# A two-layer graph network kernel: layer 0's first group by eight plain outer products instead of seven combined ones, its results in both streams' banks, and first loads in another order

## The chip, the core and the metric

The kernel runs on one core of a Trainium2 chip. The metric is device time in microseconds (us) from the first to the last instruction. Engines work side by side, each with its own queue in order, and wait for one another by semaphores: TensorE (PE, with its weight loads PEld), VectorE (DVE), ScalarE (ACT), GpSimd (POOL) and SyncE (SP), which here only issues transfers. Results of matmuls go to eight banks of PSUM, of 128 partitions by 512 float32 numbers each.

## The reference

There are 128 graphs of 128 nodes with 512 features. Layer 0 gathers neighbours, multiplies by one weight matrix and normalizes; layer 1 is a diffusion over two hops.

```
# layer 0, for each graph b
deg = sum(adj, -1);  agg = (adj @ x) / max(deg, 1e-6)
out = relu(concat([x, agg]) @ W.T)            # W is 512 x 1024
x = layernorm(x + out)
# layer 1, for each graph b
e = leaky_relu(sj + si + ab, 0.2)             # scores from x @ Wv and aw
T = adj * exp(e), rows divided by their sums
h = x @ Wk[0] + T @ (x @ Wk[1] + T @ (x @ Wk[2])) + biases   # the sum over hops, rewritten
x = layernorm(x + relu(h))
```

By linearity layer 0's product is computed as x @ W1 + adj_n @ (x @ W2), where W1 and W2 are the two halves of W.T and adj_n is the adjacency with its rows divided by the degrees.

## The kernel before

**Groups and streams.** The graphs go through in 32 groups of four (G), as two pairs p = 0, 1. Two generators emit the instructions of TensorE and their companions in steps: `stream0` is layer 0 of one group, 18 steps (NA), and `stream1` is layer 1 of one pair, 9 steps, in other banks (bA0 to bA3 for stream 0, bB0 to bB3 for stream 1). The main loop at the end of the file takes one step of each per turn t, stream 1 beginning at t = 24 (LAG). The order on all engines is the order of emission in this loop: it runs as written.

**What stands beside them.** Everything else (loads, transposes, sums, statistics, softmax) is a list of small functions with a place each: place 2t is emitted after stream 0's step t, place 2t + 1 after stream 1's. `EARLY` holds the places of group 0, `PLACES` of the middle groups, `LATE` of the last, each counted from the group's start; `START` holds what happens once (weight sums, folding of constants, the first x sums). What a step appends to `late` is emitted after the place's functions, the evictions of a last bank among them.

**Products.** Both layers' products use a fast scheme with seven products for a 2 by 2 block product (instead of eight), with sums of blocks ahead of it and additions in the banks behind it. Layer 0 uses it twice. The inner level is `prod(bank, k)` for k = 1 to 7 in the order 1, 5, 6, 2, 7, 3, 4, with the tables `LEFT` and `RIGHT` choosing the blocks. The outer level is over pairs of graphs (xu for pair 0, xl for pair 1), halves of the 512 input features, and the two column blocks W2 and W1. It also has seven products, in `outer_pair(1, 2)`, `(5, 6)`, `(7, 4)`, and product 3 by itself (49 block products in all). Its left sums are `x_s1` to `x_s4` (lines 224 to 233), its right sums `w_outer(1)` to `(4)` (line 681), its result sums `sum_s`, `sum_d`, `sum_c21`, `sum_c22` on GpSimd and VectorE. Results go to SBUF (r, s, c11, c22) and the last ones stay in the banks bA, where the products with the transposed adjacency aT (`mm(bA[...], aT[...], ...)`) are added to them. `residual` then adds relu of a bank to y.

**One product in the code.** `mm` (line 251) issues one block product of 128x128 by 128x256; the profile counts two MATMUL instructions for each, so 49 block products are 98 instructions. Between prod 1 and prod 6 ScalarE copies bank 0 to bank 1 (line 263) and bank 3 to s5 (line 265); VectorE adds s5 into bank 2 behind prod 6 (line 268) and into bank 3 behind prod 7 (line 273); TensorE's next product in bank 0 must wait for these additions to have read it.

**x and the weights.** x comes by `load_x_blocks` in 32-row blocks and is turned by VectorE in 32x32 blocks (`x_turn`, line 216), then `x_inner` makes the left inner sums in four additions (lines 202 to 205). wf holds 7 by 7 weight blocks: `load_w0(o)` fills outer index o, raw, `w_inner(p)` makes the inner sums of two outer indices (lines 196 to 199: p = 0 for blocks 0 and 2, p = 1 for blocks 1 and 3), and `w_outer` adds whole outer blocks of 128 x 1792 numbers.

**Start.** 16 matmuls on the identity (line 149) fill the banks; then the first product needs block 0 of the weights and pair 0 of x. The loads at the head of the kernel are 16 transfers of 128 KB for the weights and 8 for x of group 0. The 8 hardware semaphores for transfers are taken in turn: transfer n waits, on the queue that issues it, for transfer n - 8 to have landed. Constants of layer 1 are folded between group 0's products (`fold_constants`, lines 160 to 185; line 180 is the step on VectorE that ends in the vector `w2row`).

Of the kernel before, what the change touches and what calls it, by code (L numbers as in the profile page):

```python
# [8 lines left out]
FP = mybir.dt.float32  # L9
AF = mybir.ActivationFunctionType  # L10
ALU = mybir.AluOpType
# [5 lines left out]
def kernel(  # L17
# [38 lines left out]
    nc = tc.nc  # L56
    P = 128
    B, N, F = x.shape
    K = wk.shape[0]
    NC = F // P  # L60
    H = NC // 2
    FH = F // 2
    G = 4
    NG = B // G
# [4 lines left out]
    p1 = ctx.enter_context(tc.tile_pool(name="p1", bufs=1))  # L69
# [3 lines left out]
    small = ctx.enter_context(tc.tile_pool(name="small", bufs=4))  # L73
# [3 lines left out]
    R = 32  # L77
    Q = P // R
    xbs, adjs, ys = {}, {}, {}
# [14 lines left out]
    def load_x_blocks(g, p):  # L94
        b = g * G + 2 * p
        xbs[g, p] = p2.tile([P, 2, Q, P], FP, name="xb", tag="xb")
        load_blocks(xbs[g, p], x[b : b + 2])

    def load_adj(g):
        adjs[g] = p2.tile([P, G, N], FP, name="ag")  # L100
        nc.sync.dma_start(adjs[g], adj[g * G : (g + 1) * G].rearrange("b i j -> i b j"))


    wf = const.tile([P, 7, 7, FH], FP)
# [4 lines left out]
    ab_sb = const.tile([P, 1], FP)  # L109
    bk_sb = p1.tile([K, F], FP, name="bk_sb", tag="scr")  # L110

    def load_w0(eng, o):
        src = w0t[(F if o in (0, 2) else 0) + 0 :]
        for q in range(Q):
            r0 = q * P + (o // 2) * H * R
            eng.dma_start(wf[q * R : (q + 1) * R, o, :4].rearrange("s (c n) m -> s c (n m)", c=H),
                          src[r0 : r0 + H * R].rearrange("(c s) o -> s c o", s=R))

    load_w0(nc.scalar, 0)
    load_x_blocks(0, 0)  # L120
    load_w0(nc.sync, 2)
    load_w0(nc.scalar, 1)
    load_x_blocks(0, 1)
    load_w0(nc.scalar, 3)
    load_adj(0)
    for i in range(2):
        nc.sync.dma_start(wvt_sb[i], wvt[i * FH : (i + 1) * FH, :].rearrange("(c p) f -> p c f", p=P))
# [18 lines left out]
    bA = [psum.tile([P, F], FP, name=f"bA{i}") for i in range(4)]  # L146
    bB = [psum.tile([P, F], FP, name=f"bB{i}") for i in range(4)]
# [43 lines left out]
    LEFT = [None, 0, 1, 6, 3, 4, 5, 2]  # L191
    RIGHT = [None, 0, 2, 3, 6, 4, 5, 1]
# [8 lines left out]
    def left_sums(eng, t):  # L201
        eng[0].tensor_add(t[4], t[2], t[3])  # L202
        eng[1].tensor_sub(t[2], t[0], t[2])
        eng[2].tensor_sub(t[5], t[4], t[0])  # L204
        eng[3].tensor_sub(t[6], t[1], t[5])

    V, S_, L_ = nc.vector, nc.gpsimd, nc.scalar


    xu = const.tile([P, 2, 7, P], FP)  # L210
    xl = const.tile([P, 2, 7, P], FP)
    xs = const.tile([P, 2, 7, P], FP)

    def x_turn(g, p, i):
        t, src = (xu, xl)[p], xbs[g, p]
        V.transpose(t[:, :, 2 * i : 2 * i + 2].rearrange("p o k (j r) -> p j o k r", r=R),
                    src[:, i].rearrange("p j (o k s) -> p j o k s", o=2, k=2))

    def x_inner(g, p):
        t = (xu, xl)[p]  # L220
        left_sums([V, V, V, V], [t[:, :, i] for i in range(7)])
# [13 lines left out]
    def left_of(i):  # L235
        return {1: xu[:, 0], 2: xu[:, 1], 3: xu[:, 1], 4: xl[:, 1], 5: xs[:, 0], 6: xs[:, 1], 7: xl[:, 0]}[i]

    def right_of(i):
        return wf[:, RIGHT[i]]
# [10 lines left out]
    def mm(dst, lhsT, rhs, start=False):  # L250
        nc.tensor.matmul(dst, lhsT, rhs, start=start, stop=True, skip_group_check=True)  # L251


    ans, aTs, ybs, yfs, scs, Ts, TTs = {}, {}, {}, {}, {}, {}, {}
# [27 lines left out]
    late = []  # L282
# [4 lines left out]
    def stream0(g):  # L287

        r = p1.tile([P, 4, FH], FP, name="r")
        c11 = p1.tile([P, 4, FH], FP, name="c11")  # L290
        s = p1.tile([P, 4, FH], FP, name="s")
        d = p1.tile([P, 3, FH], FP, name="d")
        c22 = p1.tile([P, 4, FH], FP, name="c22")
        parts[g] = r, s, d, c22

        def evict1(b):
            L_.copy(r[:, b], bA[b][:, :FH])
            V.tensor_add(c11[:, b], bA[b][:, FH:], r[:, b])
        yield from outer_pair(1, 2, evict1)

        def evict2(b):
            L_.copy(s[:, b], bA[b][:, :FH])  # L302
            V.tensor_add(r[:, b], bA[b][:, FH:], r[:, b])  # L303
        yield from outer_pair(5, 6, evict2)

        def evict3(b):
            L_.copy(c22[:, b], bA[b][:, :FH])  # L307
            V.tensor_add(r[:, b], bA[b][:, FH:], r[:, b])  # L308
        yield from outer_pair(7, 4, evict3)


        X, Y, W, Z, E = bA[2][:, :FH], bA[1][:, :FH], bA[1][:, FH:], bA[2][:, FH:], bA[3][:, :FH]
        def prod(dst, k):
            mm(dst, left_of(3)[:, LEFT[k]], right_of(3)[:, RIGHT[k]])
        s5 = p1.tile([P, 2, FH], FP, name="hs")
        L_.copy(X, s[:, 0])
        L_.copy(E, d[:, 1])
        prod(X, 1)
        V.tensor_add(Y, X, d[:, 0])
        prod(E, 5)  # L320
        L_.copy(s5[:, 0], E)
        yield
        prod(Y, 2)
        V.tensor_add(s5[:, 1], s5[:, 0], d[:, 2])
        prod(X, 6)
        V.tensor_add(W, X, s5[:, 0])
        yield
        prod(X, 7)
        V.tensor_add(Z, X, s5[:, 1])
        prod(W, 3)  # L330
        L_.copy(bA[0].rearrange("p (a m) -> p a m", a=2), c22[:, 1:3])  # L331
        yield
        prod(X, 4)
        L_.copy(bA[3].rearrange("p (a m) -> p a m", a=2), c22[:, 0:4:3])
        yield
        own, other = slice(1, 3), slice(0, 4, 3)
        aT = aTs[g]
        mv = mvs[g] = small.tile([P, G, 2], FP, name="mv")
        def residual(b, k):
            y = ys[g, b // 2][:, b % 2]  # L340
            V.scalar_tensor_tensor(y, bA[k], 0.0, y, ALU.max, ALU.add, accum_out=mv[:, b, 0:1])
        mm(bA[0], aT[:, 2], r[:, own])
        mm(bA[3], aT[:, 3], r[:, other])
        late.append((residual, 2, 0))
        late.append((residual, 3, 3))
        yield
        mm(bA[1], aT[:, 0], c11[:, own])
        mm(bA[2], aT[:, 1], c11[:, other])
        late.append((residual, 0, 1))
        late.append((residual, 1, 2))  # L350
        yield

    parts = {}

# [24 lines left out]
    mvs, rstds = {}, {}  # L379
# [243 lines left out]
    def x_s1_next(): pass  # L623
    nexts = {load_adj_next: load_adj, load_x_blocks_next: load_x_blocks, x_turn_next: x_turn, x_inner_next: x_inner, x_s1_next: x_s1}

    EARLY = {
        (t_load,): 42, (t_back,): 51, (y_store, 1): 43, (y_turn, 1, 0): 46, (load_x, 0): 0, (x_s4,): 6, (sum_s,): 17,
        (sum_c21,): 23, (sum_c22,): 25, (a_transpose,): 25, (load_adj_next,): 5, (load_x_blocks_next, 1): 9,
        (x_turn_next, 1, 1): 23, (x_turn_next, 0, 1): 33, (y_stats, 2): 34, (x_turn_next, 1, 0): 26, (y_stats, 3): 33,
        (y_scales, 1): 34, (y_scores, 2): 33, (o_store, 0): 90, (y_norm, 2): 35, (y_norm, 3): 35, (y_store, 2): 36,  # L630
        (t_norm,): 49, (y_store, 3): 36, (y_stats, 0): 37, (y_stats, 1): 38, (x_turn_next, 0, 0): 28,
        (y_scales, 0): 40, (y_scores, 0): 35, (y_scores, 1): 39, (y_norm, 0): 40, (y_norm, 1): 40, (y_store, 0): 41,
        (x_inner_next, 1): 30, (y_load, 0): 44, (t_scores,): 40, (t_exp,): 47, (t_sums,): 48, (t_transpose,): 55,
        (y_turn, 1, 1): 46, (y_sums, 1): 47, (y_turn, 0, 0): 57, (y_turn, 0, 1): 60, (y_sums, 0): 64,
        (o_stats, 1): 66, (o_scales, 1): 66, (o_norm, 1): 69, (o_store, 1): 72, (o_stats, 0): 84, (o_scales, 0): 87,
        (x_inner_next, 0): 33, (y_scores, 3): 33, (load_x, 1): 13, (sum_d,): 22, (y_load, 1): 38,
        (load_x_blocks_next, 0): 25, (o_norm, 0): 87, (x_s1_next,): 33,
    }
    PLACES = {
        (o_scales, 0): 87, (y_norm, 1): 42, (x_turn_next, 1, 1): 27, (o_store, 1): 73, (o_norm, 0): 87, (x_s4,): 11,  # L640
# [35 lines left out]
    def w_inner(p):  # L676
        right_sums([V, V, V, V], [wf[:, p : p + 3 : 2, i] for i in range(7)])

    def w_outer(i):
# [1 line left out]
        eng.tensor_sub(wf[:, d], wf[:, m], wf[:, n])  # L681

    START = {
        (x_turn, 0, 1, 0): 1, (x_inner, 0, 1): 2, (x_s2, 0): 5, (w_outer, 4): 10, (degree, 0): 8, (fold, 3): 2,
        (fold, 4): 15, (fold, 5): 9, (load_wk,): 11, (fold, 2): 5, (x_turn, 0, 1, 1): 1, (w_inner, 1): 0,
        (fold, 1): 6, (w_outer, 3): 12, (w_outer, 2): 3, (fold, 7): 23, (wk_sums, 0): 24, (wk_sums, 2): 45,
        (x_s1, 0): 3, (fold, 6): 5, (a_load, 0): 17, (a_norm, 0): 12, (x_s3, 0): 6, (w_outer, 1): 0,
    }
    for (f, *args), place in START.items():
        at(place, f, *args)  # L690
    for i in range(2):
        x_turn(0, 0, i)
    w_inner(0)
    x_inner(0, 0)

    def run(fs):
        while fs:
# [3 lines left out]
    def chain(gens):  # L701
        for h in gens:
            yield from h()

    a = chain([lambda g=g: stream0(g) for g in range(NG)])
    b = chain([lambda g=g, p=p: stream1(g, p) for g in range(NG) for p in (1, 0)])
    ET = mybir.EngineType
    with tc.manual_schedule(engines={ET.PE, ET.DVE, ET.Activation, ET.Pool, ET.SP}):
# [34 lines left out]
```

## Time and profile before

| | us |
|---|---|
| median of 3 runs | 2235.78 (2235.29 to 2237.61) |
| profiled execution | 2235.6 |
| PE busy | 2197.9 (98%) |
| VectorE busy | 1378.6 (62%) |
| ScalarE busy | 1060.2 (47%) |
| GpSimd busy | 690.9 (31%) |
| PE busy in the first 100 us | 75.22 |
| mean granted TensorE clock | 0.995 |

PE's busy time tells at most where it is not busy: the share says little on how well it computes. The slices of the page show where along the run an engine is short of work; the list of waits says what ended each idle time; the timeline puts these in order. In the timeline each line begins with the start and the length of a run of like instructions, and the brackets tell how long the engine was idle before it and what released it. DMA lines on a queue give the time of issue only.

### The profile page before, as it was taken

To read this page: it belongs to the slowest core of one execution; us is meant where nothing else is said; L and a number is where in the kernel's file an instruction comes from. 1 tells how busy PE (TensorE), PEld (TensorE's weight loads), DVE (VectorE), ACT (ScalarE), POOL (GpSimd) and SP (SyncE) were. 2 spreads that over 40 slices of the span, in tenths; PEclk is the share of its full clock that TensorE was granted. 3 is DMA by queue.
4 is the path that set the end of the run, shared out by engine and by line. 5 is a ranking of instruction groups with operands and counts; after the bars stand their busy time and mean duration, and the time that the engine had idled before them with its cause. 6 is when DMAs were issued, how large, how long until landed. Compare 5 with 4: busy or idle time off the path is not lost. (4 is left out here: it accounts for less than half of the span.)

```text
span 2235.6 us, 24900 instructions
## 1 busy us (share of the span) xinstructions
PE 2197.9 (98%) x7520; PEld 1424.9 (64%) x7520; DVE 1378.6 (62%) x3219; ACT 1060.2 (47%) x2438; POOL 690.9 (31%) x983
## 2 busy tenths in 40 slices
PE   7899999999999999999999999999999999999998
PEld 4566666666666666666666666666666666666654
DVE  5766665666665666665666655666656666656652
ACT  2444444544445544445545445444445544455443
POOL 3432323332322322322322232323233223223221
PEclk8999999999999999999999999999999999999999
DMA  8333344333344333344333344333443233443321
GB/s 188 95 95 98 82 104 123 110 85 103 89 105 123 104 86 89 97 117 123 93 92 87 97 123 113 90 97 88 104 123 109 81 102 92 109 123 98 87 81 47
DMA packets 392039, 226.60 MB, mean 101 GB/s; under 512 B 155357, under 2 KB 335581, under 8 KB 391904
## 3 DMA queue, kind: packets, MB, share of 16 engines
q1 hardware_dynamic: 390816, 223.43, 38.0%
q10 hardware_dynamic: 960, 1.57, 0.4%
q8 instruction: 59, 0.97, 0.2%
q14 instruction: 76, 0.62, 0.1%
q0 software_dynamic: 128, 0.01, 0.0%
HBM read 140.52 MB, written 84.41 MB: 101 GB/s over the span
## 5 line engine op out<-in xcount | busy, mean ns | idle before, releaser
L251 PE MATMUL bB<-wk_sb,yf 128*128 128x512 f32 (+1 forms) x2048 | 723.5, 486 | 3.5 <-DVE bB L550 1.7
L251 PE MATMUL bB<-t,yf 128*128 128x512 f32 (+1 forms) x1536 | 558.0, 486 | 1.0 <-ACT bB L517 1.0
L251 PEld LDWEIGHTS bB<-wk_sb,yf 128*128 128x128 f32 x2048 | 388.6, 190 | 238.6 <-issue 200.3
L251 PEld LDWEIGHTS bB<-t,yf 128*128 128x128 f32 x1536 | 291.9, 190 | 192.8 <-issue 161.1
L251 PE MATMUL bA<-wf,xu 128*128 128x256 f32 x1344 | 340.4, 386 | 15.8 <-DVE bA L268 6.4
L204 POOL TENSOR_TENSOR yf<-yf 128x256 f32<-128x256 f32 x64 | 57.8, 903 | 926.6 <-DVE yf L202 910.6
L251 PEld LDWEIGHTS bA<-wf,xu 128*128 128x128 f32 x1344 | 252.1, 192 | 119.5 <-issue 60.3
L251 PE MATMUL bA<-wf,xs 128*128 128x256 f32 x896 | 216.2, 382 | 4.9 <-DVE bA L268 3.5
L251 PEld LDWEIGHTS bA<-wf,xl 128*128 128x128 f32 x896 | 169.9, 190 | 78.9 <-issue 58.4
L251 PE MATMUL bA<-wf,xl 128*128 128x256 f32 x896 | 214.6, 380 | 1.0 <-DVE r L303 1.0
L251 PEld LDWEIGHTS bA<-wf,xs 128*128 128x128 f32 x896 | 171.1, 191 | 56.7 <-issue 28.9
L268 DVE TENSOR_TENSOR bA<-bA,hs 128x512 f32<-128x512 f32 x96 | 67.1, 699 | 190.9 <-PE bA L251 186.5
L391 DVE SCALAR_TENSOR_TENSOR scr<-y,wrow 128x512 bf16<-128x512 f32 x256 | 177.0, 691 | 5.5
L377 ACT ACTIVATE junk<-y,mvo 128x512 bf16<-128x512 f32 x128 | 92.4, 722 | 142.4 <-POOL mvo L376 136.8
L331 ACT COPY bA<-c 128x512 f32<-128x512 f32 x32 | 18.9, 590 | 250.2 <-DVE y L562 235.2
L308 DVE TENSOR_TENSOR r<-bA,r 128x256 f32<-128x256 f32 x128 | 48.4, 419 | 139.7 <-ACT c L307 137.3
L404 ACT ACTIVATE y<-y,mv,sc 128x512 f32<-128x512 f32 x128 | 104.9, 822 | 62.1 <-POOL mv L398 61.6
L251 PE MATMUL bB<-v,TT 128*128 128x512 f32 x256 | 130.8, 592 | 0.0
L562 DVE SCALAR_TENSOR_TENSOR y<-bB,y 128x512 f32<-128x512 f32 x128 | 88.0, 688 | 59.0 <-PE bB L251 58.9
L251 PE MATMUL bB<-u,TT 128*128 128x512 f32 x256 | 120.6, 593 | 0.5 <-DVE TT L501 0.5
L303 DVE TENSOR_TENSOR r<-bA,r 128x256 f32<-128x256 f32 x128 | 48.3, 418 | 116.9 <-ACT s L302 116.9
L357 POOL TENSOR_TENSOR s<-s,r 128x1024 f32<-128x1024 f32 x32 | 75.6, 2363 | 115.1 <-DVE r L303 115.1
(140 smaller groups left out, 2891.1 us busy)
## 6 DMA issues: line engine op xcount, KB each, us to landing
xb<-in_x_dram SPq DMA_DIRECT2D x256, 128.0 KB
y<-in_x_dram SPq DMA_DIRECT2D x64, 512.0 KB
yd<-y SPq DMA_DIRECT2D x128, 256.0 KB
yb<-yd SPq DMA_DIRECT2D x256, 128.0 KB
out_dram<-y SPq DMA_DIRECT2D x128, 256.0 KB
ag<-in_adj_dram SPq DMA_DIRECT2D x32, 256.0 KB
sd<-an SPq DMA_DIRECT2D x32, 256.0 KB
anb<-sd SPq DMA_DIRECT2D x128, 64.0 KB
```

What stands on the lines that cost most here:

```text
L204: eng[2].tensor_sub(t[5], t[4], t[0])
L251: nc.tensor.matmul(dst, lhsT, rhs, start=start, stop=True, skip_group_check=True)
L268: V.tensor_add(bA[2], bA[0], s5)
L303: V.tensor_add(r[:, b], bA[b][:, FH:], r[:, b])
L308: V.tensor_add(r[:, b], bA[b][:, FH:], r[:, b])
L331: L_.copy(bA[0].rearrange("p (a m) -> p a m", a=2), c22[:, 1:3])
L357: S_.tensor_add(s, s, r)
L377: L_.activation(junk, t, AF.Square, bias=mv[:, 0:1], accum_out=mv[:, 1:2])
L391: V.scalar_tensor_tensor(scr, y, 1.0, wrow[:, t], ALU.mult, ALU.mult, accum_out=scs[g][:, t, b : b + 1])
L404: L_.activation(t, t, AF.Identity, bias=mv[:, 0:1], scale=rstd)
L562: V.scalar_tensor_tensor(r, bB[1 + i], 0.0, r, ALU.max, ALU.add, accum_out=mv[:, i, 0:1])
```

## The change

Group 0 of layer 0 gets a generator of its own, `first0`, also of 18 steps. It takes eight outer products without combined sums: for each of the two column blocks (o = 0 for W2, o = 1 for W1) the products of both pairs with both halves of the features are accumulated, `prod` now being four block products (two pairs times two feature halves). A bank's left half holds pair 0, the right half pair 1. So the sums `x_s1` to `x_s4`, `sum_s`, `sum_d`, `sum_c21`, `sum_c22` are not needed for group 0, and the outer weight sums are needed from group 1 on only. Column 0 is evicted to SBUF (c11 and r); column 1 is evicted to the banks bB, which stream 1 does not use yet, and the adjacency products are added there.

The outer weight sums move to later places, and so does `w_inner(1)`. Both pairs of x are turned ahead of the loop. Of the loads, weight block 2 is split over the scalar and the sync queue, and block 1 comes after the second pair of x. Places of group 0's and group 1's other functions shift by a few steps. The purpose is to let TensorE start on raw blocks sooner, with less work of the other engines ahead of it.

```diff
-    def load_w0(eng, o):
+    def load_w0(engs, o):
...
-            eng.dma_start(wf[q * R : (q + 1) * R, o, :4].rearrange("s (c n) m -> s c (n m)", c=H),
+            engs[q % len(engs)].dma_start(wf[q * R : (q + 1) * R, o, :4].rearrange("s (c n) m -> s c (n m)", c=H),
...
-    load_w0(nc.scalar, 0)
+    load_w0([nc.scalar], 0)
     load_x_blocks(0, 0)
-    load_w0(nc.sync, 2)
-    load_w0(nc.scalar, 1)
+    load_w0([nc.scalar, nc.sync], 2)
     load_x_blocks(0, 1)
-    load_w0(nc.scalar, 3)
+    load_w0([nc.scalar], 1)
+    load_w0([nc.scalar], 3)
...
+    def first0():
+        c = [p1.tile([P, 4, FH], FP, name=n) for n in ("c11", "r")]
+
+        def outer_column(o, bank_of, evict):
+            bank = [bA[i] for i in bank_of]
+            def prod(b, k, start=False):
+                for h in range(2):
+                    for i in range(2):
+                        mm(bank[b][:, h * FH : (h + 1) * FH], (xu, xl)[h][:, i, LEFT[k]], wf[:, 2 * i + o, RIGHT[k]],
+                           start and i == h == 0)
+            s5 = p1.tile([P, F], FP, name="hs")
+            prod(0, 1, True)
+            L_.copy(bank[1], bank[0])
+            yield
+            prod(3, 5, True)
+            L_.copy(s5, bank[3])
+            yield
+            prod(0, 6)
+            V.tensor_add(bank[2], bank[0], s5)
+            yield
+            prod(1, 2)
+            yield
+            prod(0, 7)
+            evict(1, bank[1])
+            V.tensor_add(bank[3], bank[0], s5)
+            yield
+            prod(2, 3)
+            yield
+            prod(0, 4)
+            evict(3, bank[3])
+            evict(2, bank[2])
+            late.append((evict, 0, bank[0]))
+            yield
+
+        def evict0(b, t):
+            L_.copy(c[0][:, b], t[:, :FH])
+            V.tensor_copy(c[1][:, b], t[:, FH:])
+        yield from outer_column(0, (0, 1, 2, 3), evict0)
+
+        def evict1(b, t):
+            i, h = {1: (0, 0), 2: (0, 1), 0: (1, 0), 3: (1, 1)}[b]
+            L_.copy(bB[i][:, h * FH : (h + 1) * FH], t[:, :FH])
+            V.tensor_copy(bB[2 + i][:, h * FH : (h + 1) * FH], t[:, FH:])
+        yield from outer_column(1, (1, 2, 0, 3), evict1)
...
+        for p in (1, 0):
+            for i, k in enumerate((slice(1, 3), slice(0, 4, 3))):
+                b = 2 * p + i
+                mm(bB[b], aT[:, b], c[p][:, k])
+                late.append((residual, b))
+                yield
...
     START = {
-        (x_turn, 0, 1, 0): 1, (x_inner, 0, 1): 2, (x_s2, 0): 5, (w_outer, 4): 10, (degree, 0): 8, (fold, 3): 2,
-        (fold, 4): 15, (fold, 5): 9, (load_wk,): 11, (fold, 2): 5, (x_turn, 0, 1, 1): 1, (w_inner, 1): 0,
-        (fold, 1): 6, (w_outer, 3): 12, (w_outer, 2): 3, (fold, 7): 23, (wk_sums, 0): 24, (wk_sums, 2): 45,
-        (x_s1, 0): 3, (fold, 6): 5, (a_load, 0): 17, (a_norm, 0): 12, (x_s3, 0): 6, (w_outer, 1): 0,
+        (w_outer, 4): 18, (degree, 0): 12, (fold, 3): 8, (fold, 4): 11, (load_wk,): 11, (fold, 2): 5, (w_inner, 1): 5,
+        (fold, 1): 9, (w_outer, 3): 28, (w_outer, 2): 11, (fold, 7): 16, (wk_sums, 0): 24, (wk_sums, 2): 45,
+        (fold, 6): 15, (a_load, 0): 17, (a_norm, 0): 13, (w_outer, 1): 9, (fold, 5): 9,
     }
...
-    a = chain([lambda g=g: stream0(g) for g in range(NG)])
+    a = chain([lambda g=g: stream0(g) if g else first0() for g in range(NG)])
```

Of the places of `EARLY`, these move: `x_turn_next` of pair 1 from 26 and 23 to 22 and 28 (halves 0 and 1), the second one of pair 0 from 33 to 31, `x_inner_next(1)` from 30 to 29, `y_scores` of graphs 0 and 1 from 35 and 39 to 38, `y_norm(3)` from 35 to 36.

More of the change, by code (lines that the diff above doesn't have):

```diff
@@ L351, in stream0, with residual @@
         yield
+    def first0():
[39 more added lines that the diff above has]
+        yield from outer_column(1, (1, 2, 0, 3), evict1)
+        aT = aTs[0]
+        mv = mvs[0] = small.tile([P, G, 2], FP, name="mv")
+        def residual(b):
+            y = ys[0, b // 2][:, b % 2]
+            V.scalar_tensor_tensor(y, bB[b], 0.0, y, ALU.max, ALU.add, accum_out=mv[:, b, 0:1])
+        for p in (1, 0):
[4 more added lines that the diff above has]
+                yield
     parts = {}
@@ L626 @@
     EARLY = {
[L627 to L637, printed above, removed]
+        (t_load,): 42, (t_back,): 51, (y_store, 1): 43, (y_turn, 1, 0): 46, (load_x, 0): 0, (a_transpose,): 25,
+        (load_adj_next,): 5, (load_x_blocks_next, 1): 9, (x_turn_next, 1, 1): 28, (x_turn_next, 0, 1): 31,
+        (y_stats, 2): 34, (x_turn_next, 1, 0): 22, (y_stats, 3): 33, (y_scales, 1): 34, (y_scores, 2): 33,
+        (o_store, 0): 90, (y_norm, 2): 35, (y_norm, 3): 36, (y_store, 2): 36, (t_norm,): 49, (y_store, 3): 36,
+        (y_stats, 0): 37, (y_stats, 1): 38, (x_turn_next, 0, 0): 28, (y_scales, 0): 40, (y_scores, 1): 38,
+        (y_norm, 0): 40, (y_norm, 1): 40, (y_store, 0): 41, (x_inner_next, 1): 29, (y_load, 0): 44, (t_scores,): 40,
+        (t_exp,): 47, (t_sums,): 48, (t_transpose,): 55, (y_turn, 1, 1): 46, (y_sums, 1): 47, (y_turn, 0, 0): 57,
+        (y_turn, 0, 1): 60, (y_sums, 0): 64, (o_stats, 1): 66, (o_scales, 1): 66, (o_norm, 1): 69, (o_store, 1): 72,
+        (o_stats, 0): 84, (o_scales, 0): 87, (x_inner_next, 0): 33, (y_scores, 3): 33, (load_x, 1): 13,
+        (y_load, 1): 38, (load_x_blocks_next, 0): 25, (o_norm, 0): 87, (x_s1_next,): 33, (y_scores, 0): 38,
     }
@@ L692 @@
         x_turn(0, 0, i)
+    for i in range(2):
+        x_turn(0, 1, i)
+    x_inner(0, 0)
+    x_inner(0, 1)
     w_inner(0)
-    x_inner(0, 0)
     def run(fs):
```

## The prediction, on record before the run

> **What bounds the kernel now.** I read the granted clock of the core (0.995), then the busy rows by slice, then TensorE's waits, then the timeline of the first 100 us. The rows of the page (tenths of 55.9 us slices):
>
> ```profile
> PE   7899999999999999999999999999999999999998
> PEclk8999999999999999999999999999999999999999
> ```
>
> TensorE is short of full only in the first two slices and the last. Asked by window, TensorE's waits from 100 to 2100 us are none, and from 2100 us on they sum to 4.8 us. In the first 100 us it idles 24.8 us (busy 75.22). So the kernel is TensorE-bound but for its start, and a microsecond won before 100 us moves the end by a microsecond. Waits of the whole run (total, times, longest):
>
> ```profile
> PE bA L251 <- DVE bA L268: 9.9, 2, 6.4
> PE bA L251 <- ACT bA L263: 4.0, 1, 4.0
> ```
>
> TensorE's timeline (start, length, instructions, idle before and its releaser):
>
> ```profile
> 13.35 3.70 PE L251 MATMUL bA<-wf,xu 128*128 128x256 f32 x14 [1.40 <-DMA wf<-in_w0t_dram]
> ...
> 24.49 3.78 PE L251 MATMUL bA<-wf,xu 128*128 128x256 f32 x8 [6.39 <-DVE bA L268]
> ...
> 63.90 1.88 PE L251 MATMUL bA<-r,aTt 128*128 128x512 f32 x4
> ...
> 74.21 6.46 PE L251 MATMUL bA<-wf,xu 128*128 128x256 f32 x20 [4.04 <-ACT bA L263]
> 82.09 1.13 PE L251 MATMUL bA<-wf,xs 128*128 128x256 f32 x4 [1.42 <-DVE c L298]
> ```
>
> Group 0's aggregation starts at 63.90, group 1's second pair at 82.09; from there only 0.97 us is lost up to 2150. These two times are my marks. VectorE's timeline gives the cause:
>
> ```profile
> 17.95 0.69 DVE L196 TENSOR_TENSOR wf<-wf 128x512 f32<-128x512 f32 x1 [1.99 <-DMA wf<-in_w0t_dram]
> ...
> 22.55 1.30 DVE L216 STREAM_TRANSPOSE xl<-xb 128x512 f32<-128x512 f32 x2
> 23.77 0.67 DVE L268 TENSOR_TENSOR bA<-bA,hs 128x512 f32<-128x512 f32 x1
> ...
> 39.36 3.27 DVE L180 TENSOR_SCALAR w2row<-w2row,wm 2x512 f32<-2x512 f32 x1
> ```
>
> The addition that TensorE awaits at 24.4 stood behind the sums of weight blocks 1 and 3, whose loads land at 17.95, behind the outer sum of line 681 (2.02) and two transposes. From 62.9 to 82.0 VectorE does not rest: the windows 60-70 and 70-80 show it 9.65 and 9.60 of 10 us busy, TensorE only 7.26 and 5.96.
>
> **What the Trainium skill says.** "TensorE: Matmul & The Clock Gate", What's actually happening: an idle window of about 3.4 us halves TensorE's clock and a busy one restores it. The trace agrees on the first and is worse on the second: after the 6.39 us wait the clock is 0.50 from 25 to 33.3, the 8 instructions take 0.47 us each, and some 4.3 us are lost; after the 4.04 us wait the 20 instructions take 6.46 instead of 4.9. "SBUF — State Buffer", Who interferes with whom: a VectorE instruction with two SBUF inputs, or in a two-port mode, waits until a running GpSimd instruction ends. It agrees: line 180's 3.27 us ends with GpSimd's 3.96 us sum of 38.39. "DMA: Bandwidth & Descriptors", Issuing engines are not separate DMA queues: a second queue saves issue time only. Here eight loads are in flight and each issue waits for the eighth before it, so the order decides what lands first.
>
> **The change part by part.**
>
> *TensorE's work.* 8 products of 7 block products instead of 7: 56 against 49, two instructions each. 28 such took 6.81 us (48.81 to 55.62), 0.243 each: 14 more are +3.4 us, fully on TensorE's path. The adjacency products keep 4 pairs of instructions.
>
> *Loads.* In before the third block of 4 loads (weight block 2, all on the sync queue) was issued from 4.42 to 8.72 and landed by 13.3, so an issue takes some 4.5 us to land. Now two of these go on the scalar queue, whose next slots were 4.07 and 5.6: block 2 lands near 10.5. The second x pair then takes sync's slots 7.5, 8.7, 10.1 and 10.9 and lands near 15.4 (10.9 + 4.5). The scalar queue gets 14 issues for 12; its last reuses a slot of the x pair, so it ends near 15.5 instead of 13.1. The table load (1.28) follows: ScalarE's first copy can run from 17.0, before that nothing asks for it. Blocks 1 and 3 land near 20, and are wanted only by column 1 of the weights.
>
> *Start.* TensorE does half the first product at 11.5, behind its warm-up, then waits for the second x pair: 15.4 + 1.3 (two transposes) + signal = 16.9. From there to group 0's aggregation: (112 - 4) instructions x 0.243 = 26.2; the folding matmuls between them 0.95 + 0.5 + 3.6 + 2.1 = 7.15 (lines 160, 168, 173, 184 at full clock); half clock after 4.4 us idle, between 1.6 and 4.4 us by the two cases above, taken as 3.0. Sum 36.4, so aggregation starts at **53.3** instead of 63.9, 10.6 earlier.
>
> *Waits inside that stretch.* The first addition into bank 2 (line 268 in before) now stands behind nothing but x sums. Blocks 1 and 3 are summed after it, while TensorE has 2 products of 1.94. The outer sums (VectorE 2.0, GpSimd 2 x 3.96) begin near 31 and end near 41; their readers, group 1's second pair, come at 76. Line 180 can be caught again: it is free when the first GpSimd sum ends near 37, TensorE wants it near 39; if it slips behind the second, 41, which costs 1.4 us. Degree, normalization, adjacency round trip: the normalized adjacency is written near 43, at 41.4 before; its loads back were issued by 45.9, so now by 47.5, and wait 4.5 to land: 52.0, when VectorE's transpose comes to them. Moving group 0's last products from half banks to whole ones takes out lines 316 to 329 and their waits (0.95, 0.21, 1.97), which are inside the 10.6.
>
> *VectorE behind it.* Its queue is in order, and behind the last eviction (0.5 after TensorE's last product, 53.8) the new order has, by before's rows: transposes 2 x 0.63, the outer sum w_outer(3) 1.93, residual 0.61, sums of xl 1.56, residual 0.61, transpose 0.63, residual 0.61, two scores 1.38, sums of xu 1.59, two scores 1.35, line 224 1.0: 12.5, plus residual 0.6 to 66.9. From 66.3 GpSimd runs line 227 for 2.08 (to 68.4), then group 0's statistics go between GpSimd and ScalarE as before, where 7.28 us passed from the end of line 227 (74.81) to 82.09. 68.4 + 7.3 = 75.7. Straight down VectorE's queue the same point comes to: 66.9, addition 0.6, four scores with the port wait 3.3, eviction and addition 1.0, scores' turn 0.6, line 230 1.0, three evictions 1.1, some 74.5 without waits. TensorE needs just 56.7 + 28 x 0.243 = 63.5, so it waits for VectorE; its clock falls meanwhile, which is hidden. I add 0.9, between nothing and twice that, for xu's sums arriving only at 62.5 and ScalarE's normalization standing ahead of its bank copy: second pair at **76.6** for 82.09, 5.5 earlier. So of 10.6 us about half is handed back: w_outer(3) and a second transpose of xl (2.6 us) were done ahead of the marks before, and now stand in the full queue.
>
> *Rest.* From the second pair on the same instructions stand in the same order, with the y loads, exponentials and their waits moving along. The group loops behind are unchanged, so 2235.8 - 5.5 = **2230.3**.
>
> **The rivals.**
> (A) As above, VectorE's queue after group 0 sets the end: 2230.3, chance 0.60. For it: 9.6 of 10 us busy there, and 22 us of work in order.
> (B) All passes: scores and statistics slide behind TensorE's need, 2235.8 - 10.6 = 2225.2, chance 0.15. For it: the 4.04 us wait falls away for certain, since group 0's residuals now read the other four banks. Against: xs of line 230 and the evictions stand behind the scores in the order.
> (C) TensorE comes late: half clock as long as before (1.4 more), line 180 caught by the second GpSimd sum (1.4), the x pair 1.0 later; 3.8 off the gain, 2234.1, chance 0.17.
> (D) New waits at each step keep the clock at half through column 0: its 52 remaining instructions and 5.05 us of folding, 17.7 us of work, then take 17.7 us more, not 3.0, and 5.5 - 14.7 = -9.2: 2245, slower, chance 0.08. For it: the clock stayed at half for 8 us of busy work in before; against: it came back there without any pause.
>
> **How the numbers follow.** The range 2225 to 2235 holds A, B and C with their unknowns (clock, port wait, landing); it leaves out D and the tails. The bound is 4.5 us. A's gain has a spread of some 1.5, so about 0.13 of its 0.60 falls within the bound: faster 0.47 + 0.15 = 0.62, same 0.13 + 0.17 = 0.30, slower 0.08.
>
> **What would show it.** Aggregation on bank bB near 53 and group 1's second pair near 76.6; the first matmul on xl near 17, released by VectorE's transpose; one run of half clock of 3 to 9 us behind it; no wait on line 268 or 263 of 4 us or more before 50; TensorE idle from 57 to 76 by some 9 us, released by VectorE; no wait from 100 to 2100. Wrong: an x pair landing after 17, a wait for wrow or the adjacency, or a VectorE queue that drains before 75.

## The result, and the profile after

| | before | changed |
|---|---|---|
| median of the first runs, us | 2235.53 (2235.22 to 2237.61, 4 runs) | 2228.45 (2227.59 to 2229.24, 4 runs) |
| profiled execution, first to last instruction on the core, us | 2235.6 | 2226.0 |
| the same execution as the medians time it, us | 2237.41 | 2227.72 |
| PE busy in the first 100 us | 75.22 | 84.00 |
| mean granted clock (share of TensorE's full speed) in the first 100 us | 0.90 | 0.93 |

The ratio is 0.9963, with a 95% interval of 0.9949 to 0.9978: the change makes the kernel faster, by 7.1 us by these medians and by 9.6 us between the two profiled executions. The two figures differ because the profiled execution of before took 1.9 us more than its median and that of the changed kernel 0.7 us less than its own; the marks below come from these two executions, so they show more than the medians. The predicted time was 2230.3, the range 2225 to 2235. On the chip of experiments 3 and 10 the same kernel took 2227.98 beside 2237.80 for the kernel before (ratio 0.9959, interval 0.9946 to 0.9973).

The slices of the page. The first one rises, and the second is full as far as a tenth can tell:

```profile
PE   8899999999999999999999999999999999999998
...
PEclk9999999999999999999999999999999999999999
```

TensorE's waits over the whole run (total, times, longest). The 6.4 us for line 268 and the 4.0 us for line 263 are gone; in their place stand waits that are new or shorter:

```profile
PE bA L251 <- DVE xu L202: 4.6, 1, 4.6
PE bA L251 <- DVE xl L216: 3.6, 1, 3.6
...
PE bA L251 <- DVE bA L273: 2.0, 1, 2.0
PE bA L251 <- DVE c L298: 2.0, 1, 2.0
...
PE bB L251 <- DVE bB L397: 0.8, 1, 0.8
```

TensorE's timeline, with the two marks of the prediction in it (start, length, instructions, idle before and releaser). The first line is the start on the second x pair, the fourth the aggregation, the sixth group 1's second pair:

```profile
16.43 1.22 PE L251 MATMUL bA<-wf,xl 128*128 128x256 f32 x4 [3.59 <-DVE xl L216]
17.44 1.91 PE L251 MATMUL bA<-wf,xu 128*128 128x256 f32 x4
...
48.59 1.03 PE L251 MATMUL bA<-wf,xl 128*128 128x256 f32 x4
50.43 1.98 PE L251 MATMUL bB<-r,aTt 128*128 128x512 f32 x4 [0.82 <-DVE bB L397]
...
59.59 7.54 PE L251 MATMUL bA<-wf,xu 128*128 128x256 f32 x20 [4.59 <-DVE xu L202]
...
72.23 7.24 PE L251 MATMUL bA<-wf,xs 128*128 128x256 f32 x24 [1.97 <-DVE c L298]
```

| mark | before | predicted | changed | earlier by |
|---|---|---|---|---|
| aggregation of group 0 starts | 63.90 | 53.3 | 50.43 | 13.5 |
| group 1's second pair starts | 82.09 | 76.6 | 72.23 | 9.9 |
| end | 2235.6 | | 2226.0 | 9.6 |

So 13.5 us were won up to the aggregation, and 3.6 of them were given back in the next 22 us. From 100 to 2100 us TensorE waits for nothing in either kernel, and its waits at the end are 4.8 and 4.9 us: what is won at the second pair stays won, but for the small changes of the next 15 us.

VectorE's timeline behind the aggregation shows where the 3.6 us went:

```profile
49.01 0.71 DVE L511 STREAM_TRANSPOSE aTt<-anb 128x512 f32<-128x512 f32 x1 [1.50 <-DMA anb<-sd]
49.65 1.06 DVE L397 COPY bB<-bA 128x256 f32<-128x256 f32 x3
...
51.84 1.98 DVE L739 TENSOR_TENSOR wf<-wf 128x1792 f32<-128x1792 f32 x1
...
63.96 0.70 DVE L268 TENSOR_TENSOR bA<-bA,hs 128x512 f32<-128x512 f32 x1 [0.21 <-PE bA L251]
...
71.09 1.09 DVE L298 TENSOR_TENSOR c<-bA,r 128x256 f32<-128x256 f32 x3 [0.43 <-ACT r L297]
```

In between there is no bracket of importance: VectorE is busy for 16.98 of the 18 us from 54 to 72, TensorE for 9.56. The last eviction (line 298, ended at 72.2) releases the second pair.

### The profile page after: what moved, and what is told of

It is laid out like the page before. It is cut to its first block, busy times and chain, and to the rows that moved or that the text cites. A ratio compares the mean times of both kernels' runs of the same rounds, so it can differ in the third digit from the quotient of the medians.

```text
span 2226.0 us, 24892 instructions
## 1 busy us (share of the span) xinstructions
PE 2197.0 (99%) x7534; PEld 1427.7 (64%) x7534; DVE 1367.5 (61%) x3206; ACT 1055.9 (47%) x2427; POOL 679.8 (31%) x977
## 5 line engine op out<-in xcount | busy, mean ns | idle before, releaser
L251 PEld LDWEIGHTS bA<-wf,xl 128*128 128x128 f32 x924 | 176.0, 191 | 81.1 <-issue 57.2
L251 PE MATMUL bA<-wf,xl 128*128 128x256 f32 x924 | 223.0, 380 | 3.6 <-DVE xl L216 3.6
L251 PE MATMUL bA<-wf,xs 128*128 128x256 f32 x868 | 209.1, 381 | 2.0 <-DVE c L298 2.0
L251 PEld LDWEIGHTS bA<-wf,xs 128*128 128x128 f32 x868 | 165.8, 191 | 51.6 <-issue 29.2
L583 ACT COPY u<-bB 128x512 f32<-128x512 f32 x64 | 37.5, 586 | 148.6 <-PE bB L251 148.6
```

Source lines behind the costliest of these rows:

```text
L583: L_.copy(u[:, 0], Y)
```

## The experiments

In each the time is a median, with the ratio to the kernel before on the same chip; the marks are from its profiled execution. Of long lines of the tables of places only the entries that change are shown. The experiments ran on three chips, on which the kernel before took 2237.0 to 2237.8, and the changed kernel was timed on one of these only; where two versions differ by about 1 us, the times alone are weak evidence, and the marks have to carry it. The kernel before spreads more than the changed one: 2234.8 to 2240.2 over all its runs, against 2227.6 to 2229.2. Where its mean clock is 0.993 or 0.994 its time is 2238 to 2239.4, where it is 0.995 or 0.996 it is 2234.8 to 2237.9 (the eleven runs beside experiments 3 and 10). That stretches of half clock differ from run to run is an inference for this kernel, of which there is one trace; of the changed kernel there are two (experiment 10), and there they do.

**1. The changed kernel with the old order of loads.**

```diff
-    load_w0([nc.scalar, nc.sync], 2)
+    load_w0([nc.sync], 2)
+    load_w0([nc.scalar], 1)
     load_x_blocks(0, 1)
-    load_w0([nc.scalar], 1)
```

> The changed kernel with the first loads in the order of before (weight block 2 wholly on the sync queue, block 1 ahead of the second x pair); the rest as changed. Theory 1 (the second x pair's landing sets the start and everything behind it to the end moves with it): the pair lands near 17.7 instead of 15.6, the first matmul on xl starts near 18.5 instead of 16.4, group 1's second pair near 74.3 instead of 72.2, time 2230.5. Rival (the delay is absorbed in VectorE's queue or in the adjacency round trip that group 0's aggregation waits for): second pair within 0.5 of 72.2, time 2228.5.

Measured: 2231.32 (ratio 0.9972, interval 0.9962 to 0.9982). TensorE's timeline of this kernel:

```profile
19.07 2.07 PE L251 MATMUL bA<-wf,xl 128*128 128x256 f32 x4 [5.34 <-DVE xl L216]
...
53.44 2.26 PE L251 MATMUL bB<-r,aTt 128*128 128x512 f32 x4
...
76.04 7.40 PE L251 MATMUL bA<-wf,xs 128*128 128x256 f32 x24 [1.97 <-DVE c L298]
```

The start is 2.6 us later, the aggregation 3.0, the second pair 3.8. VectorE's transposes of the second x pair begin 2.6 us later as well (18.30 instead of 15.66): the landing of this pair sets the start, and the delay goes through. In the changed kernel the load order is worth some 3 us. The rest of the change, without it, keeps 6.1 us (2237.39 before, 2231.32 here). No run splits this rest, so how much is due to the plain products and how much to the results in bank bB is open.

**2. The kernel before with only its sums in another order.**

```diff
-        (x_turn, 0, 1, 0): 1, (x_turn, 0, 1, 1): 1, (x_inner, 0, 1): 2, (w_inner, 1): 0,
-        (w_outer, 1): 0, (w_outer, 2): 3, (x_s1, 0): 3,
+        (x_turn, 0, 1, 0): 2, (x_turn, 0, 1, 1): 2, (x_inner, 0, 1): 2, (w_inner, 1): 2,
+        (w_outer, 1): 4, (w_outer, 2): 4, (x_s1, 0): 4,
```

> The kernel before (seven combined outer products, old loads) with only the order of VectorE's first work changed: the addition into bank 2 first, then pair 1's transposes and inner sums, then the inner sums of weight blocks 1 and 3, then the outer weight sums. Theory 1 (the combined products themselves need the outer sums early, so order alone helps little): the 6.4 us wait goes, but the second outer pair waits for the outer sums on VectorE and GpSimd until about 32.5 instead of 36.0; 2 to 3.5 us are won, time near 2232.5. Rival (the order of the sums was the whole trouble): 7 us are won, time near 2228.5.

Measured: 2236.98, ratio 0.9999 (0.9991 to 1.0007): nothing. TensorE's timeline of this kernel:

```profile
34.67 6.38 PE L251 MATMUL bA<-wf,xs 128*128 128x256 f32 x16 [5.74 <-DVE c L298]
...
63.41 2.18 PE L251 MATMUL bA<-r,aTt 128*128 128x512 f32 x4
...
73.84 6.47 PE L251 MATMUL bA<-wf,xu 128*128 128x256 f32 x20 [4.05 <-ACT bA L263]
```

The 6.4 us wait is gone, but the next combined pair waits 5.74 us instead. The named releaser is an eviction that stands behind the outer sum (2.02) and the x sum of line 230 in VectorE's order, and that x sum ran beside GpSimd's outer sum:

```profile
27.55 4.73 POOL L681 TENSOR_TENSOR wf<-wf 128x1792 f32<-128x1792 f32 x1 [23.34 <-DVE wf L681]
...
28.49 4.73 DVE L230 TENSOR_TENSOR xs<-xs,xu 128x896 f32<-128x896 f32 x1
```

It took 4.73 us, ended 0.94 behind that sum, and took 1.08 in before: by these figures an estimated 3.7 of the 5.74 us come from this meeting. 1.3 us are won at this pair, 0.5 at the aggregation. Theory 1 was right in kind and too generous in size: in this place too the outer sums are ahead of the combined pair. The run shows that this order wins nothing, not that no order could.

**3. The kernel before with only the new order of loads.** The edit is that of the change's loads alone.

> The kernel before (seven combined products, its order of sums) with only the new order of the first loads. Theory 1 (the new load order pays only with plain products, since the combined ones need weight blocks 1 and 3 at once and these now land later): the first addition that TensorE waits for comes 1 to 2 us later, time 0.5 to 2 above before. Rival (the load order is worth its 3 us by itself): 3 us faster than before.

Measured: 2243.80, ratio 1.0026 (1.0015 to 1.0036): 6 us *slower*. TensorE's timeline of this kernel:

```profile
17.86 3.78 PE L251 MATMUL bA<-wf,xu 128*128 128x256 f32 x8 [4.58 <-ACT bA L263]
...
28.51 3.78 PE L251 MATMUL bA<-wf,xu 128*128 128x256 f32 x8 [4.87 <-DVE bA L268]
```

ScalarE issues 14 loads and then its table load, so its first copy runs at 17.2 instead of 14.4; the sums of weight blocks 1 and 3 begin at 21.97 instead of 17.95, so the awaited addition stands at 27.79 instead of 23.77. With these two waits of over 4 us the clock is 0.50 from 16.1 to 36.5; in before its mean over the same stretch is 0.67. Five of the seven runs took 2243.7 to 2244.1, all at a mean clock of 0.991, the other two 2239.4 and 2241.8 at 0.995 and 0.994, so the half clock is likely a large part of the loss. The order that is worth 3 us with plain products costs 6 with combined ones: neither it nor the order of sums of experiment 2 is worth anything without plain products. The direction was as theory 1 had it, the size three times its upper figure.

**4. w_outer(3) behind group 1's first pair.**

```diff
-        (w_outer, 3): 28,
+        (w_outer, 3): 43,
```

> The changed kernel with the outer weight sum w_outer(3), 1.9 us of VectorE, moved from behind group 0's last eviction to behind group 1's first outer pair. Theory 1 (VectorE's queue in order after group 0 sets the end): group 1's second pair starts 1.9 earlier, near 70.3 instead of 72.2, and the time falls by 1.9 to 2226.5. Rival (statistics on GpSimd and ScalarE, or TensorE itself, set it): second pair within 0.4 of 72.2, time 2228.4.

Measured: 2227.23 (ratio 0.9956, 0.9943 to 0.997), so 0.8 us less than the changed kernel's 2227.98, not 1.9. TensorE's timeline of this kernel:

```profile
69.96 7.15 PE L251 MATMUL bA<-wf,xs 128*128 128x256 f32 x24 [1.97 <-DVE c L298]
...
86.11 1.99 PE L251 MATMUL bA<-wf,xl 128*128 128x256 f32 x8 [1.27 <-DVE r L303]
```

The second pair starts 2.3 us earlier. Of these, 1.9 lie behind the aggregation, as VectorE's queue has it (from mark to mark 19.86 us, from 50.10, instead of 21.80); 0.3 were won ahead of it, where this execution shows no half clock at the start. Then 1.3 us go into a wait that the changed kernel does not have. It is for an eviction behind the normalization of the transition matrices on ScalarE, which waits for VectorE's sums.

**5. In addition, that normalization behind the eviction.**

```diff
+    def t_norm_behind(g):
+        late.append((t_norm, g))
-        (t_norm,): 49,
+        (t_norm_behind,): 50,
```

> The kernel with w_outer(3) moved late (2227.2), and in addition ScalarE's normalization of the first transition matrices put behind the eviction of group 1's second pair instead of ahead of it. Theory 1 (of the 2.3 us that moving w_outer(3) won at the second pair, 1.3 were given back at the third pair, whose first product waits for an eviction that stands behind this normalization): that 1.3 us wait goes, time 2226.0. Rival (the delay comes back further on, at the transposed transition matrix): time within 0.3 of 2227.2.

Measured: 2226.10 (ratio 0.9953), second pair at 70.28, and no TensorE wait from there to 2100. As expected: 1.1 us less than in experiment 4. The third pair, which waited there, starts at 85.25 instead of 86.11.

**6. The longest wait taken away, the work unchanged.**

```diff
-        (x_turn_next, 0, 1): 31, (x_inner_next, 0): 33,
+        (x_turn_next, 0, 1): 28, (x_inner_next, 0): 28,
```

> The changed kernel with pair 0 of the next group turned and summed ahead of group 0's residuals and scores on VectorE, so that TensorE's longest wait (4.6 us for xu) has nothing to wait for; VectorE's work is the same. Theory 1 (the chain residuals, statistics, normalization and VectorE's queue as a whole set group 1's second pair, not any one wait): the 4.6 us wait goes and another takes its place, for ScalarE's bank copy behind the normalization; second pair within 0.5 of 72.2 and time within 0.5 of 2228.4. Rival (the wait for xu is the bound): second pair 3 to 4 earlier, time 2224.5.

Measured: 2229.20 (ratio 0.9966). TensorE's timeline of this kernel:

```profile
64.59 5.32 PE L251 MATMUL bA<-wf,xu 128*128 128x256 f32 x16 [9.22 <-ACT bA L263]
...
73.81 5.83 PE L251 MATMUL bA<-wf,xs 128*128 128x256 f32 x24 [1.42 <-DVE c L298]
```

The 4.6 us wait for xu is gone and one of 9.2 us stands in its place: ScalarE's bank copy comes behind the statistics and normalization of group 0 in its queue, and these come later by the work that was put ahead of the residuals. The second pair is 1.6 us later. The longest wait was not the bound. The expectation that mark and time stay within 0.5 failed: the time is 0.8 above 2228.4. The first residual on VectorE starts at 55.84 instead of 53.74, and the copy runs at 63.96 instead of 61.15: this speaks for the chain of residual, statistics and normalization, and not only the sum of VectorE's work, as what counts.

**7. The adjacency early.**

```diff
-        (degree, 0): 12, (a_norm, 0): 13,
+        (degree, 0): 6, (a_norm, 0): 12,
```

> The changed kernel with the adjacency's degree sums six places earlier (ahead of the outer weight sums on VectorE) and its normalization one place earlier, so that it is back before VectorE comes to its transpose. Theory 1 (VectorE's wait for the adjacency, 1.5 us until 49.0, holds the last evictions and so the aggregation and all behind it): no such wait, TensorE's 0.82 us wait ahead of the aggregation nearly gone, aggregation near 49.6 instead of 50.4, second pair near 71.4, time 2227.6. Rival (the last eviction waits for TensorE in any case and the queue behind it is the same): within 0.3 of 2228.4.

Measured: 2227.31 (ratio 0.9957), 0.7 less than the changed kernel, which is within the spread of both (its runs are 2225.8 to 2228.1); the marks carry this one. TensorE's timeline of this kernel:

```profile
48.95 2.26 PE L251 MATMUL bB<-r,aTt 128*128 128x512 f32 x4
...
71.53 8.38 PE L251 MATMUL bA<-wf,xs 128*128 128x256 f32 x24 [1.96 <-DVE c L298]
```

VectorE's 1.5 us wait is gone, the aggregation starts at 48.95 (1.5 earlier), the second pair at 71.53 (0.7 earlier). The adjacency's round trip was on the path; half of what it frees is given back to the queue.

**8. Filler in the wait for the second x pair.** Four products with the identity, which nobody reads, keep TensorE busy there.

```diff
+                    if k == 1 and o == h == 0:
+                        for _ in range(4):
+                            nc.tensor.matmul(bB[1], ident, ident[:, None, :].to_broadcast([P, Q, P]), start=True, stop=True)
```

> The changed kernel with four matmuls on the identity (eight instructions, some 3.5 us of TensorE work in a bank not yet in use) while TensorE waits for the second x pair. Theory 1 (the half clock behind that wait is on the path): no half clock from 16.4 to 20.8, 1.8 us are won at the start and again at group 1's second pair (70.4), time near 2226.7. Rival (the adjacency round trip, on which VectorE waits until 49.0 ahead of the last evictions, sets the start of the aggregation): column 1 ends earlier but the aggregation starts within 0.5 of 50.4, time 2228.2.

Measured: 2227.85 (ratio 0.9958), within the spread of the changed kernel. TensorE's timeline of this kernel:

```profile
16.49 1.13 PE L251 MATMUL bA<-wf,xl 128*128 128x256 f32 x4 [0.70 <-DVE xl L216]
...
49.81 1.98 PE L251 MATMUL bB<-r,aTt 128*128 128x512 f32 x4 [1.82 <-DVE bB L400]
```

The instructions behind the wait run at full clock, so column 1 ends 1.6 us earlier, but the wait for the adjacency in front of the aggregation grows to 1.82 us and it starts at 49.81: nearly the rival's outcome (0.6 earlier, where the rival had at most 0.5). Experiment 4 shows the same without filler: its clock stayed at 1.00 at the start, and the wait in front of its aggregation is 2.16 us.

**9. Everything together (the edits of experiments 4, 5, 7 and 8), and the same without the filler.**

> All that was found together: the changed kernel with w_outer(3) late, the transition matrices' normalization behind the eviction, the adjacency early, and the four filler matmuls in the wait for the second x pair. Theory 1 (each removes a wait from the one path): the gains add up, 1.2 + 1.2 + 0.8 and 1 us of half clock, time near 2224.5. Rival (they overlap): 2226.0.

> The kernel of all findings together (2224.0) without the filler matmuls. Theory 1 (the half clock behind the wait for the second x pair is on the path once the adjacency no longer is): 1 to 1.8 us slower, time near 2225.3. Rival (the filler gives nothing here either): within 0.3 of 2224.0.

Measured: 2223.97 with the filler (ratio 0.9943, interval 0.9931 to 0.9956), 2225.41 without (0.9948, 0.9935 to 0.996). TensorE's timeline of the full one:

```profile
16.62 1.13 PE L251 MATMUL bA<-wf,xl 128*128 128x256 f32 x4 [0.96 <-DVE xl L216]
...
47.61 2.25 PE L251 MATMUL bB<-r,aTt 128*128 128x512 f32 x4
...
68.27 3.84 PE L251 MATMUL bA<-wf,xs 128*128 128x256 f32 x16 [1.97 <-DVE c L298]
```

The aggregation starts 2.8 us ahead of the changed kernel's, the second pair 4.0. Theory 1 held: the gains add up. With the adjacency no longer in the way the same filler that gave nothing alone gives 1.4 us by the medians, on two chips, and 1.7 at both marks:

```profile
49.27 2.26 PE L251 MATMUL bB<-r,aTt 128*128 128x512 f32 x4
...
69.92 3.84 PE L251 MATMUL bA<-wf,xs 128*128 128x256 f32 x16 [1.96 <-DVE c L298]
```

These two lines are from the version without filler. The full version is 4.0 us faster than the changed kernel's 2227.98 and 13.1 us faster than the kernel before beside it (2237.03).

**10. The changed kernel once more.**

> The changed kernel again, unaltered, so that it is timed beside before on a chip of the experiments. Both theories: the difference to before is 8 to 9 us, the mean of what the first runs (7.1 by medians) and the two profiled executions (9.6) show; the time is near 2228.4.

Measured: 2227.98, 9.8 us under before by medians, 9.2 by the ratio of 0.9959. Expected was 8 to 9: slightly over by medians. Its marks repeat those of the first trace (50.56 and 72.36), but the half clock falls elsewhere: the 24 instructions behind the second pair take 8.35 us instead of 7.24, at a clock of 0.64 instead of 0.79 from 72 to 80, and the core ends at 2227.2 instead of 2226.0.

## Why the prediction was right, point by point

- **The frame.** Right: only the first 100 us can give anything, and from 100 to 2100 TensorE waits for nothing in both kernels. Of the rivals, A's path came true (VectorE's queue busy for 17 of 18 us, then the second pair), and its size was low: 5.5 predicted, 7.1 to 9.8 measured. That 2230.3 came so near 2228.45 is in part luck: at the second pair the prediction was 4.4 us off (76.6 against 72.23). It had taken its marks from an execution of before that was 1.6 us slower than the 2235.8 from which it took off its gain, and the profiled execution of the changed kernel was 0.7 us faster than its median.
- **Start.** 16.9 predicted, 16.43 measured; first copy of ScalarE at 17.69, its table load from 15.95. Load order and the 14 issues were read rightly, and experiment 1 shows that the start hangs on them.
- **From the start to the aggregation: 36.4 predicted, 34.0 measured.** Four terms were mis-sized. *Products*: 108 instructions at 0.243 are 26.2; they took 24.0 beside the half clock (0.223 each; a stretch of four that follows others of its kind takes 0.87, so 0.217 each). In the row of before that gave 0.243 TensorE's weight loads wait three times, for ScalarE's copy (0.25) and VectorE's additions (0.39 and 0.33); between these joints the instructions start 0.216 apart there too. In the changed kernel the 40 instructions from 40.71 to 49.45 have no such wait. *Half clock*: 3.0 taken, 1.75 measured (12 instructions from 16.43 to 20.81 against 2.63). *Folding*: 7.15 taken, 6.9 measured. *Waits*: none taken, 1.3 measured, of which 1.0 is the adjacency. 24.0 + 1.75 + 6.9 + 1.3 is 34.0.
- **Adjacency.** Its landing was put at 52.0, when VectorE would come to it. Column 1 came sooner, and 49.0, when it did land, was late for it: the wait for the adjacency, which the prediction names as a sign of being wrong, did come, and cost 1.0 us. What was overlooked is the port that VectorE and GpSimd share: the degrees' step on line 495, 128x4 numbers, took 2.49 us, from 36.16 until the second outer sum on GpSimd ended at 38.64, and the normalization waits for it. That GpSimd would catch line 180 at the first sum, not the second, was right: it took 2.84 us and ended at 34.8. The Trainium skill, "SBUF — State Buffer", Who interferes with whom, says that a VectorE instruction with two inputs in SBUF contends with a GpSimd instruction that reads SBUF, that `tensor_scalar` can do so in a two-port mode, and that the lock is exclusive. Line 495 is of the first kind, line 180 is a `tensor_scalar`. The trace agrees: line 180 ended 0.3 us behind the first GpSimd sum, line 495 with the second:

```profile
30.55 8.09 POOL L739 TENSOR_TENSOR wf<-wf 128x1792 f32<-128x1792 f32 x2 [26.35 <-DVE wf L739]
...
31.96 2.84 DVE L180 TENSOR_SCALAR w2row<-w2row,wm 2x512 f32<-2x512 f32 x1
...
36.16 2.49 DVE L495 TENSOR_TENSOR deg<-deg,eps 128x4 f32<-128x4 f32 x1
...
38.90 1.28 ACT L503 ACTIVATE an<-ag,rdeg 128x128 f32<-128x128 f32 x4 [3.81 <-DVE rdeg L497]
```

- **Handing back.** 10.6 to 5.5 predicted, 13.5 to 9.9 measured. The cause is, for about half of the 3.6 us, the one that was named: experiment 4 takes the 1.98 us of w_outer(3) out of the full queue and shortens the way from mark to mark by 1.9. That the second transpose makes up part of the rest fits the queue, but no run tests it. The 0.9 us added for late xu sums was not needed: from the end of line 227 on GpSimd (65.36) to the second pair passed 6.9 us, not 7.3 and 0.9.
- **Behind the second pair.** That the same instructions stand in the same order was right, that their waits just move along was not quite. The 24 instructions took 7.24 us against 5.83 in before, with the clock at 0.70 from 70 to 75 after the waits ahead of them. On the other side a wait of 0.97 us for line 303 fell away. The two nearly cancel: 9.9 us at the second pair are 9.6 at the end.
- **Rival D** did not come: one stretch of half clock, between 16.4 and 20.8, then full clock to 54. Nor did C: the half clock cost less than was taken, line 180 met the first sum, and the x pair came 0.5 us sooner than predicted. Rival B (nothing handed back) would have been 13.5, and is not seen.

## What to carry to other kernels

A part of a change can be worth less than nothing by itself: neither the load order (6 us slower alone) nor the one other order of sums that was tried (nothing) helps the combined products, while with plain products, at 14 more instructions on the bounding engine, the whole wins 7 to 10 us. Where another engine's queue in order sets the next start, take work out of that queue; here, taking away the bounding engine's longest wait made a wait twice as long in its place. Follow a gain from mark to mark: the single findings lost half or more at the next bound, and added up when that bound was moved too.

## What the runs showed of the hardware that was not expected

- With filler matmuls in the wait for the second x pair (experiments 8 and 9) the granted clock was 1.00 from 11 to 25 us; without them it was 0.88 in the two traces of the changed kernel, after waits of 3.59 and 4.29 us, but 1.00 in experiment 4 as well, after a wait of 3.13. Whether it shows in the time depended on the next wait: 0.1 us alone, 1.4 us with the adjacency out of the way.
- The half clock is part of the run-to-run spread: the kernel before took 2234.8 to 2239.4 on one chip, at mean clocks from 0.996 down to 0.993, and the two traces of the changed kernel differ by 1.1 us in one stretch of 24 instructions. The full version of experiment 9 spread by 1.2 us over five runs.
- A VectorE step on 128x4 numbers, 0.62 us in before and 0.20 in experiment 2, took 2.49 us beside a GpSimd sum, and in experiment 2 a sum on 128x896 numbers took 4.73 instead of 1.08.
